# A GRU, attention and AUGRU kernel: the GRU phase in written order, attention taken out a step later, one softmax for both halves

## The chip, the cores and the metric

The kernel runs on one core of a Trainium2 chip. The metric is the device time of one execution in microseconds (us). The kernel before takes 2262.76 us, the median of 3 runs (2262.09 to 2263.09).

## What is computed

A recommendation model for 1024 users (B), each with a history of 100 items (T) of 128 numbers (D), a 0/1 mask and a length between 1 and 100. Everything is float32. Cut to its core, with `sig` for the sigmoid:

```python
hist_sum = (x * mask[:, :, None]).sum(1) / length          # [B, D]
for t in range(T):                                          # GRU over the history
    r, z = sig(Wr x_t + Ur h + b), sig(Wz x_t + Uz h + b)
    n = tanh(Wn x_t + b + r * (Un h + b'))
    h = (1 - z) * n + z * h;  keys[:, t] = h
feat = [keys, q, keys - q, q * keys]                        # q: the item, for all t
score = mlp(feat, 512 -> 80 -> 40 -> 1, relu)               # relu after each layer
attn = softmax(where(mask == 1, score, -inf), over t)
pooled = sum_t attn[:, t] * keys[:, t]                      # [B, 128]
att_seq = pooled.T[:T]                                      # the weight of step t is pooled[:, t]
for t in range(T):                                          # AUGRU over the keys
    r, u = sig(Wr [h, k_t] + b), sig(Wu [h, k_t] + b)
    c = tanh(Wh [h * r, k_t] + b)
    u = att_seq[t] * u;  h = (1 - u) * h + u * c;  seq[:, t] = h
out = mlp([user, q, hist_sum, q * hist_sum, seq[:, length - 1]], 640 -> 200 -> 80 -> 1, sig)
```

The AUGRU weights of a user depend on the pooled keys of the whole history, so no AUGRU step can begin before the last GRU step, its attention score and the last softmax are done.

## The kernel before

The users are two halves of 512. A tile is [128 features, 512 users]. A float32 matmul shows as two matmul instructions in the trace.

**GRU phase** (`gru_phase`, with one `Half` object for each half). The loop over the 100 steps issues for each half: the loads of x (`load`, L434) and of the broadcast mask row (`load_mask`, L439) for two steps ahead on SP's queue; `gru` (gates on PE at L463: r, the state part of n, the input part of n, z; ACT at L475, L480, L494; DVE at L483 to L498); `product` (L530: state times item) and `transpose` (L507: the state into rows of users, stored to DRAM as keys at L513 or L518) of the step before; after the second half `attend` of the step before; one pending softmax stage; `history` (L450, L451: GpSimd adds x times mask); and `pool` (L619, L620 on GpSimd: keys times exponents, added up, two keys a call).

`attend(t)` packs the three layers of the score network of three different steps into one PSUM tile of each half (L679, 32-column matmuls beside each other): layer 1 of step t, layer 2 of t-1, layer 3 of t-2. At once behind it DVE adds the item's part (L703), ACT applies relu (L704) and `score` sends the score row from ACT's queue to the score tile `s_b` (L540).

The softmax runs over blocks of steps (`ENDS`, mostly 8 steps, shifted by 4 between the halves, the last block 2 steps) with a running maximum `top` and sum `den`. Its two stages per half (`scores`: transpose, mask, maximum, Exp on ACT at L579; `sums`) are queued and one is issued after each half's step. An old block's pooled sum is rescaled at L605.

`load_later` is a generator; from step 2 on one piece of it is issued per step. It makes the mask tables, the lengths, the rank of each user by length (L347), the scatter of the ranks (L359), the index tables, and loads the AUGRU weights. In these pieces a conversion or a comparison on DVE often stands right behind the transfer that brings its input.

After the loop come `attend(T)` and `attend(T + 1)` for the last layers, the last stages, the rest of the pooling, `weights` (L629 to L635: pooled sums divided by `den`, stored to `pooled_d`), and `features` (L641 to L664: the parts of the last network that need no AUGRU).

**The order of the instructions.** The kernel is written for a scheduler: it takes the program as a graph and chooses each engine's order itself, by its own simulated times. Each engine then runs its list strictly in order; a wait holds all that stands behind it.

**AUGRU phase** (`augru_phase`). The users are sorted by length, longest first, so step t needs only the first `widths[t]` columns of each half: 512 at step 1, about 5 fewer each step, down to 16 (WIDTHS[0]; two wider tables stand in branches for other data). Keys are gathered from DRAM in the sorted order on GpSimd's queue (L128 for steps 0 to 7, L152 for later ones, paced by a copy of a gate at L151, `RATE` = 2 per half and step) in groups of 8 steps, and transposed on PE (L819) or DVE (L823). `sort_weights` gathers the pooled rows (L128 `att_r`), transposes them (L789) and stores them (L792); `load_att` reads back a broadcast row for a step (L806). `step` (L834, L835 on PE; L840 to L848 on ACT; L841 to L851 on DVE) uses gate tiles from a ring of 8 in PSUM; `predict` runs the last network for 128 users whenever they have finished.

## Time and profile before

| | us |
|---|---|
| the profiled execution | 2262.48 |
| its span (first to last instruction) | 2260.6 |
| PE matmuls busy | 2124.9 |
| DVE busy | 1728.9 |
| GpSimd (POOL) busy | 1285.2 |
| ACT busy | 868.3 |
| mean granted TensorE clock | 0.96 of full |

By stretches of the span: the GRU phase reaches to about 1530, the change-over to about 1602 (first matmul of AUGRU step 1), the AUGRU steps to 2247, the last network to 2261.

How to read it: "PE" is the matrix engine, "PEld" its weight loads, "DVE" VectorE, "ACT" ScalarE, "POOL" GpSimd and "SP" the engine whose queue issues most transfers. A name such as `ps<-x,wih` says that a tile `ps` is written from `x` and `wih`. Busy time on PE is not work at full speed: at a granted clock of 0.5 the same matmuls take longer and still count as busy. In the table of stretches each engine has its busy time and, in brackets, its instructions; then come the granted clock, the mean busy share of the transfer engines and GB/s. In the waits, "A <- B: us, times, longest" says that engine A stood idle until B; a wait for several events is put down to the last.

### The profile page before, as it was taken

Reading aid. Unit: us, or ns where it says so; the run is one execution under the profiler, and the core shown is the slowest. Engines: PE = TensorE matmul, PEld = TensorE weight load, DVE = VectorE, ACT = ScalarE, POOL = GpSimd, SP = SyncE. Lnnn points to the kernel's source line nnn. Section 1 sums busy time; section 2 is a strip of 40 time slices with the busy share of each in tenths; the row PEclk is TensorE's granted clock in tenths of the full one; section 3 lists DMA queues with packets and bytes.
Section 4 is the critical chain, followed back from the end, with each engine's and each line's share of the span. In section 5 each row is a group of like instructions: output and inputs, shape, how many; then the busy total and the mean of one; then the engine's idle time right before and its main releaser. Section 6 shows DMA issues by size and latency. Waiting matters only on the chain. (4 is left out here: it accounts for less than half of the span.)

```text
span 2260.6 us, 26532 instructions
## 1 busy us (share of the span) xinstructions
PE 2124.9 (94%) x8260; PEld 1013.4 (45%) x8260; DVE 1728.9 (76%) x3166; ACT 868.3 (38%) x1545; POOL 1285.2 (57%) x1289
## 2 busy tenths in 40 slices
PE   8898688999999999999999999995899999999998
PEld 3333233333333333333333333332444555679888
DVE  6776667788888888787878787898467877879752
ACT  3233223343433334333333333442343444445542
POOL 0147597676767676767676767694544444443410
PEclk9999899999999999999999999998899999999975
DMA  5344433332332323232323233312533333333310
GB/s 116 64 90 129 127 94 108 99 96 86 95 92 84 105 70 115 74 115 71 109 78 98 77 94 90 92 45 72 149 93 108 97 89 98 101 96 80 82 37 5
DMA packets 253427, 204.64 MB, mean 91 GB/s; under 512 B 74727, under 2 KB 215755, under 8 KB 253275
## 3 DMA queue, kind: packets, MB, share of 16 engines
q1 hardware_dynamic: 239482, 169.03, 27.7%
q0 software_dynamic: 12192, 32.17, 4.9%
q10 hardware_dynamic: 1600, 1.64, 0.2%
q8 instruction: 67, 1.10, 0.2%
q14 instruction: 86, 0.70, 0.1%
HBM read 146.73 MB, written 54.40 MB: 89 GB/s over the span
## 5 line engine op out<-in xcount | busy, mean ns | idle before, releaser
L463 PE MATMUL ps<-x,wih 128*128 128x512 f32 x1200 | 604.1, 613 | 62.2 <-ACT r L475 29.0
L463 PE MATMUL ps<-hn,whh 128*128 128x512 f32 x1188 | 583.2, 600 | 1.3 <-DVE hn L498 1.3
L463 PEld LDWEIGHTS ps<-x,wih 128*128 128x128 f32 x1200 | 220.0, 192 | 396.1 <-issue 214.1
L463 PEld LDWEIGHTS ps<-hn,whh 128*128 128x128 f32 x1188 | 228.4, 193 | 294.0 <-issue 267.6
L704 ACT ACTIVATE mv<-f 128x512 f32<-128x512 f32 (+1 forms) x204 | 128.2, 629 | 495.3 <-DVE f L703 371.7
L450 POOL TENSOR_TENSOR xm<-x,m 128x512 f32<-128x512 f32 x200 | 249.1, 1262 | 102.1 <-PE ps L463 72.6
L494 ACT ACTIVATE ps<-ps,bih 128x512 f32<-128x512 f32 x200 | 132.2, 661 | 400.7 <-DVE ps L493 324.4
L620 POOL TENSOR_TENSOR pooled<-pooled,kw 128x512 f32<-128x512 f32 x190 | 262.9, 1383 | 6.9
L451 POOL TENSOR_TENSOR hist<-hist,xm 128x512 f32<-128x512 f32 x200 | 263.7, 1333 | 2.9
L496 DVE TENSOR_TENSOR d<-hn,ps 128x512 f32<-128x512 f32 x198 | 135.7, 685 | 165.4 <-ACT ps L494 161.5
L605 POOL TENSOR_TENSOR pooled<-pooled,e 128x512 f32<-128x512 f32 x25 | 29.8, 1193 | 366.4 <-ACT e L579 366.4
L679 PE MATMUL pm<-hn,wk 128*32 128x512 f32 x1200 | 230.5, 600 | 6.0 <-DVE f L703 3.4
L152 POOL DMA_INDIRECT rows<-keys_d,idx_k x204 | 196.3, 962 | 69.3 <-issue 35.5
L679 PE MATMUL pm<-kq,wkq 128*32 128x512 f32 x1200 | 227.4, 594 | 0.0
L679 PE MATMUL pm<-mv,w 128*32 128x512 f32 (+1 forms) x808 | 213.5, 606 | 13.4 <-ACT mv L704 10.6
L530 DVE TENSOR_TENSOR kq<-hn,item 128x512 f32<-128x512 f32 x200 | 205.9, 1035 | 4.5 <-PE pm L679 4.3
L619 POOL TENSOR_TENSOR kw<-kt,e 128x512 f32<-128x512 f32 x190 | 207.4, 1110 | 0.5 <-DVE old L586 0.3
L483 DVE SCALAR_TENSOR_TENSOR u<-ps,bhh,r 128x512 f32<-128x512 f32 x198 | 145.8, 737 | 62.9 <-ACT r L475 53.7
L151 POOL COPY rows<-u 128x1 f32<-128x1 f32 x200 | 30.7, 181 | 258.4 <-DVE u L845 257.9
L497 DVE TENSOR_TENSOR d<-ps,d 128x512 f32<-128x512 f32 x200 | 137.9, 689 | 16.0 <-ACT ps L480 0.9
L493 DVE TENSOR_TENSOR ps<-ps,u 128x512 f32<-128x512 f32 x200 | 138.9, 694 | 13.5 <-PE ps L463 0.5
L835 PE MATMUL ph<-r,wh 128*128 128x512 f32 (+55 forms) x396 | 137.1, 430 | 9.5 <-DVE r L841 7.9
(154 smaller groups left out, 3167.0 us busy)
## 6 DMA issues: line engine op xcount, KB each, us to landing
x<-in_hist_x SPq DMA_DIRECT2D x212, 256.0 KB
keys_d<-kt SPq DMA_DIRECT2D x46, 1024.0 KB
m<-mask_d SPq DMA_DIRECT2D x200, 128.0 KB
keys_d<-kt SPq DMA_DIRECT2D x64, 64.0 KB
rows<-keys_d,idx_k POOLq DMA_INDIRECT x204, 2.8
s_b<-mv ACTq DMA_DIRECT2D x200, 8.0 KB
mask_i<-in_mask SPq DMA_DIRECT2D x8, 200.0 KB
at<-att_d SPq DMA_DIRECT2D x4, 256.0 KB
```

Source lines behind the costliest of these rows:

```text
L152: nc.gpsimd.indirect_dma_start(out=r[:, k, :], out_offset=None, in_=keys_d[q], in_offset=bass.IndirectOffsetOnAxis(ap=idx_k[:, k, i : i + ...
L450: nc.gpsimd.tensor_mul(d, x, m)
L451: nc.gpsimd.tensor_add(acc, acc, d)
L463: nc.tensor.matmul(p, lhsT=w[:, g, :], rhs=v, start=(j == 0), stop=(j == len(parts) - 1),)
L483: nc.vector.scalar_tensor_tensor(out=u, in0=ph, scalar=bhh[:, 2:3], in1=r, op0=ALU.add, op1=ALU.mult,)
L493: nc.vector.tensor_add(pi, pi, u)
L497: nc.vector.tensor_mul(d, pz, d)
L530: nc.vector.tensor_mul(kq, h, item[:, self.cols])
L619: eng.tensor_mul(d, k, w)
L620: eng.tensor_add(acc, acc, d)
L679: nc.tensor.matmul(p[i][s, :], lhsT=w[:, s], rhs=v, start=start, stop=stop)
L835: nc.tensor.matmul(p, lhsT=m[:, 0, :], rhs=v, start=False, stop=True)
```

## The change

**Order.** The GRU phase is put under `tc.manual_schedule()`: each engine gets its instructions in the order in which they are written. The AUGRU phase is still scheduled. The loop is rewritten for that order: `gru` calls `after_gate` behind the first gate of the first half and `after_sum` behind the tanh; z's sigmoid stands behind the tanh.

**Attention a step later.** `attend(t)` only issues the matmuls. `take(t)`, one step later, adds the item's part for both halves, applies relu and sends the score rows, now from SP's queue.

**Softmax of both halves at once.** One list of blocks (ends 8, 16, ... 88, 92, 96, 100) for both halves, three stages in three steps: the first half's scores; the second's scores, the maxima and differences; the sums. The Exp is issued at the end of the step. The last block has 4 steps.

**Preparation.** The attention weights are made after step 0. `load_later` starts with step 1, issues a piece only in steps without a softmax stage, and puts a piece's transfer and its use into different steps; conversions move from DVE to ACT, `ident` into a later piece.

**Change-over.** rlen and user are loaded two steps before the end; the cross features are made on GpSimd in step 99; the 8 feature groups stand between the last attention layers. Half 1's remaining keys are pooled on DVE, half 0's last block is split: 11 of 16 column blocks on GpSimd, 5 on DVE. The weights are built in the score tiles. In AUGRU the keys of steps 0 and 1, the first step's gates and step 1's input matmuls come before `sort_weights`. One or two keys a call are pooled in the loop; the history of steps 0 to 5 is made up from step 24 on instead of 12.

**AUGRU.** Gates use 6 PSUM tiles, everything else 2 of its own. The gathers of a group are spread evenly over the steps before it and end a step early (`spread`, for `RATE`). No width is below 96 (`LEAST`).

```diff
-ENDS = ((*range(8, 89, 8), 92, 96, 98, T), (*range(4, 93, 8), 96, 98, T))
+ENDS = (*range(8, 89, 8), 92, 96, T)
-RATE = 2
-EIGHTH, FALL = 8, 41
+EIGHTH, FALL, LEAST = 8, 41, 96
+    [max(LEAST, min(HB, 2 * -(-r // (2 * EIGHTH)))) for r in room] for room in ROOM
...
             def gru(self, t, after_gate, after_sum):
                 nc.scalar.activation(r, pr, AF.Sigmoid, bias=brz[:, 0:1])
+                after_gate()
...
-                nc.scalar.activation(pz, pz, AF.Sigmoid, bias=brz[:, 1:2])
...
                 nc.scalar.activation(pi, pi, AF.Tanh, bias=bih[:, 2:3])
+                nc.scalar.activation(pz, pz, AF.Sigmoid, bias=brz[:, 1:2])
+                after_sum()
...
+        def take(t):
+            p = left.pop(t)
+            for half in halves:
+                if t < T:
+                    sums.append(wp.tile([P, HB], F32, name="f"))
+                    nc.vector.tensor_add(sums[-1], p[half.i], q0[:, half.cols])
+            for half in halves:
+                    nc.scalar.activation(to, sums[half.i], AF.Relu)
...
+            for half in halves:
+                nc.sync.dma_start(out=s_bs[...], in_=half.mv[SC[half.i] : SC[half.i] + 1, :]...)
+            if s == blocks[j + 1] - 1:
+                softmax()
...
         for s in range(T):
+            def after_gate():
+                take(s - 2)
+                for half in halves:
+                    half.product(s - 1)
+            for half in halves:
+                half.gru(s, after_gate if s and half.i == 0 else nothing,
+                    (lambda: half.transpose(s - 1)) if s else nothing)
+                if half.i == 0:
+                    staged = bool(soft["stages"])
+                    stage(2 if last else 1)
+            exponents()
+            if s == 0:
+                attention_weights()
+            else:
+                if not staged:
+                    next(rest, None)
+                attend(s - 1)
...
+        cut = KH // 3
+        parts = (
+            ((nc.gpsimd, slice(cut, KH)), (nc.vector, slice(0, cut))),
+            ((nc.vector, slice(0, KH)),),
+        )
...
-        ps = pools.enter_context(tc.tile_pool(name="ps3", bufs=8, space=PSUM))
+        ps = pools.enter_context(tc.tile_pool(name="ps3", bufs=6, space=PSUM))
+        pa = pools.enter_context(tc.tile_pool(name="pa3", bufs=2, space=PSUM))
...
         for i in range(NH):
+            load_key(1, i)
+            open_gates(1, i)
+        for i in range(NH):
             sort_weights(i)
...
-                for _ in range(RATE):
+                for _ in range(due.pop(0) if due else 0):
                     next(ahead, None)
...
-    with ExitStack() as pools:
+    with ExitStack() as pools, tc.manual_schedule():
         gru_phase(pools)
```

More of the change, by code (lines that the diff above doesn't have):

```diff
@@ L742, in gru_phase, with some @@
+        all_of(rest)
+        features = [half.features(g) for half in halves for g in range(GH)]
+        def some(these):
+            for f in these:
+                next(f)
+        halves[0].pool(T, pool_part)
+        take(T - 2)
         for half in halves:
             half.product(T - 1)
+        attend(T - 1)
+        some(features[:2])
+        for half in halves:
             half.transpose(T - 1)
-        attend(T - 1)
-        for half in halves:
-            while half.stages:
-                half.stage()
@@ L749, in gru_phase @@
[L749 to L759 removed]
+        halves[1].pool(1, (nc.vector, slice(0, KH)))
+        take(T - 1)
+        some(features[:2])
+        attend(T)
+        some(features[2:4])
+        halves[1].pool(1, (nc.vector, slice(0, KH)))
```

530 lines of the change are left out of this document (296 added, 234 removed).

## The prediction

> **What bounds the kernel now.** I read the page first, then stretches of the span by engine, then the pace of single steps, then the waits.
>
> ```profile
> span 2260.6 us, 26532 instructions
> PE 2124.9 (94%) x8260; PEld 1013.4 (45%) x8260; DVE 1728.9 (76%) x3166; ACT 868.3 (38%) x1545; POOL 1285.2 (57%) x1289
> ...
> PE   8898688999999999999999999995899999999998
> ...
> PEclk9999899999999999999999999998899999999975
> ```
>
> TensorE is the busiest engine everywhere. There are two kinds of exceptions: the first seven slices and the 28th and 29th, where PE waits, and the last two, where PE looks nearly full but the granted clock falls. The profiled execution took 2262.48 us, 1.88 outside its span; the median of the runs is 2262.76, so the sum is made on 2260.6 and 1.88 is added at the end.
>
> The stretches; 41.89, 447.19 and 1529.47 are the starts of the attention groups of steps 1, 24 and 98, the later ones are ends or clock changes of the AUGRU phase:
>
> ```profile
> core 0: us, PE busy (x) PEld busy (x) DVE busy (x) ACT busy (x) POOL busy (x), PEclk, DMA share, GB/s
> 41.89:447.19 405.30, 353.16 (x1305) 133.31 (x1304) 288.33 (x443) 129.12 (x199) 233.27 (x192) 0.93 0.42 103
> 447.19:1529.47 1082.28, 1059.88 (x4145) 404.49 (x4145) 899.89 (x1378) 420.03 (x649) 763.24 (x616) 1.00 0.31 89
> 694.72:765.06 70.34, 70.34 (x281) 27.07 (x280) 60.50 (x94) 28.07 (x44) 40.07 (x33) 1.00 0.32 95
> 1529.47:1602.49 73.02, 43.36 (x180) 21.44 (x180) 46.15 (x106) 20.39 (x37) 37.96 (x34) 0.78 0.27 74
> 2168.07:2181.30 13.23, 11.14 (x89) 10.09 (x87) 8.10 (x44) 6.00 (x22) 0.00 (x0) 1.00 0.09 22
> 2181.30:2246.85 65.55, 64.06 (x287) 61.59 (x286) 22.55 (x140) 20.08 (x74) 2.23 (x4) 0.50 0.04 9
> 2246.85:2260.63 13.78, 5.33 (x21) 4.03 (x20) 0.00 (x1) 2.35 (x7) 1.97 (x2) 0.50 0.03 7
> ```
>
> And the pace of one GRU step, from the start of one attention group on PE to the next (timeline):
>
> ```profile
> 796.12 0.62 PE L679 MATMUL pm<-hn,wk 128*32 128x512 f32 x2
> ...
> 810.19 0.62 PE L679 MATMUL pm<-hn,wk 128*32 128x512 f32 x2
> ...
> 1529.47 0.62 PE L679 MATMUL pm<-hn,wk 128*32 128x512 f32 x2 [1.43 <-DVE e L569]
> ```
>
> An undisturbed step takes 14.07 us. A step issues 56 matmuls (24 at L463, 32 at L679). The second stretch holds 4145, that is 74 steps; the first holds 1305, of which 16 belong to `count` (L272), that is 23 steps. At 14.07 they would take 1041.2 and 323.6. The excess is 41.1 us in the second and 81.7 in the first, 122.8 together. The third row is five clean steps: PE is busy throughout, DVE 60.50/5 = 12.1 us a step, POOL 8.0. So PE's own work is the floor, and the excess is time in which PE lacked an input.
>
> What it lacked, from the waits, one row of ACT's timeline, and the waits of SP's queue between 200 and 260:
>
> ```profile
> ACT mv L704 <- DMA m<-mask_d: 82.8, 19, 5.9
> ...
> 238.50 0.63 ACT L704 ACTIVATE mv<-f 128x512 f32<-128x512 f32 x1 [14.52 <-DMA len_k<-in_len_i]
> ...
> SPq L434 <- POOL xm L450: 32.0, 4, 13.8
> ```
>
> ACT does no loads of x or masks, yet it waits for their transfers: it issues the score transfer (L540), and that issue stands in ACT's queue until an earlier transfer has ended. In the row of 238.50 this held ACT, and with it the gates, for 14.5 us.
>
> **The change, part by part.** *GRU in program order.* Inside a step no matmul is added or removed, so the floor stays 14.07. The score transfers go from ACT's queue to SP's. Behind them on SP stand the next step's x and mask loads, which are issued two steps before use, about 28 us; a score transfer waits only for a relu early in its step. I expect no one to miss them. ACT then queues arithmetic only. DVE's queue becomes, per step: two sums of the attention taken out, two products, then for each half gate product, sum, transpose of the last step, three state operations. The new waits are those at its head (the attention group of the step before, which PE has just ended) and those for ACT. Queued behind are the states of both halves; PE works in order through 12 gate matmuls a half and the attention group (14.07 shared over 24 gate matmuls and 32 that run four abreast is 0.44 each, an estimate: 5.3 us a half, 3.5 the group), so it needs each half's state some 6 to 7 us after DVE makes it. So a DVE lag of some 6 us costs nothing. Durations:
>
> ```profile
> L530 DVE TENSOR_TENSOR kq<-hn,item 128x512 f32<-128x512 f32 x200 | 205.9, 1035 | 4.5 <-PE pm L679 4.3
> L619 DVE TENSOR_TENSOR kw<-kt,e 128x512 f32<-128x512 f32 x8 | 5.5, 684 | 2.8 <-POOL pooled L620 2.8
> L619 POOL TENSOR_TENSOR kw<-kt,e 128x512 f32<-128x512 f32 x190 | 207.4, 1110 | 0.5 <-DVE old L586 0.3 <-DVE e L582 0.2
> L620 POOL TENSOR_TENSOR pooled<-pooled,kw 128x512 f32<-128x512 f32 x190 | 262.9, 1383 | 6.9
> L450 POOL TENSOR_TENSOR xm<-x,m 128x512 f32<-128x512 f32 x200 | 249.1, 1262 | 102.1 <-PE ps L463 72.6 <-DMA over_d<-over_i 19.3 <-DMA m<-mask_d 5.7
> L475 ACT ACTIVATE r<-ps,brz 128x512 f32<-128x512 f32 x200 | 136.3, 681 | 24.3 <-PE ps L463 23.9
> L579 ACT ACT_TABLE_LOAD x26 | 33.4, 1283 | 27.0 <-DVE e L574 26.7
> L272 PE MATMUL count<-alive,ones 128*1 128x100 f32 x16 | 2.8, 371 | 4.8 <-DVE own L339 4.8
> ```
>
> DVE has 14.07 - 12.1 = 2 us a step to spare, and a later softmax stage (two transposes and small operations, about 2.3) overruns by well under 6. POOL per step: history four operations of about 1.3 = 5.2, pooling of one key a half 2 x (1.11 + 1.38) = 5.0, so 10.2 of 14.07; two keys a half make 15.2, in one step of eight and again from step 92. Its lag at step 99 is then some 10 us, and the cross features (four more, 5 us) now stand in its queue ahead of half 0's last pooling; both lie under the attention layers of the change-over, and would add up to 10 us there if those were quicker. *Softmax of both halves at once* halves the 26 Exp table loads (1.28 each) and sets them behind the step's last gate on ACT; before, they stood between gates. *The preparation* issues a transfer in one step and uses it in the next, with its conversions on ACT, so DVE no longer stands before a transfer. The attention weights are made after step 0, where DVE and PE meet them in order: step 1's attention about 1 us later. I keep 7 of the 122.8 us (`count` 2.8, this 1, the rest an estimate): **-116**. Ends: -122.8 (all goes) and -75 (41.1 + 7 stays).
>
> *The change-over.*
>
> ```profile
> 1577.31 6.58 SPq L635 DMA_DIRECT2D pooled_d<-att  x8
> ...
> 1586.17 2.08 PE L777 MATMUL pu<-k,wu 128*128 128x512 f32 x2 [12.62 <-ACT k L820]
> ...
> 1586.21 0.99 POOL L128 DMA_INDIRECT att_r<-pooled_d,idx  x1 [28.03 <-DMA pooled_d<-att]
> ...
> 1604.36 0.66 PE L835 MATMUL pr<-h,wr 128*128 128x512 f32 x1
> ...
> 1616.80 0.69 DVE L851 TENSOR_TENSOR h<-h,ph 128x512 f32<-128x512 f32 x1
> ```
>
> Now it is 1586.21 - 1529.47 = 56.7 us from the start of attention step 98 to the first gather of the sorted weights, and 31.3 more to the end of AUGRU step 1. After the change the features fill PE while the last attention layers wait for each other, and the last softmax covers both halves: from the start of step 98's group I count 3.5 for it, 5 for the last state, relu and product, 3 x about 5 for the layers and their sums, 6 for transfer, scores and sums: about 30. But the last block has 4 steps, not 2. DVE pools half 1 with 9 operations of 0.68 to 1.04, 6.1 to 9.4, beside POOL's share of half 0 (11 of 16 columns of 1.1 + 4 x 2.5, 7.6), then 5/16 of 9 operations and two products, 3.5; then about 4.5 from the last store to the gather as now. That makes 44 to 47.5. The row kq, beside a busy POOL, takes 1.035 where L619 on DVE, with POOL idle, takes 0.684, so I take the slower end.
>
> The Trainium skill, GPSIMD Engine Reference, section Specifications, says why: GpSimd shares SBUF interfaces with VectorE and collides with DVE instructions that read two SBUF inputs; this speaks against pooling on both at once, and by it the 9 operations cost 3.2 us more than alone; the two rows agree.
>
> So the gather comes about 9 us sooner. Keys of steps 0 and 1 and step 1's three input matmuls a half no longer wait (row 1586.17), but PE comes back at the low clock: 5 us of the 31.3. **-14**, ends -4 (stores late, cold clock) and -22.
>
> *AUGRU.* Gate slots go from 8 to 6, exactly one step's gates, with prediction on 2 of its own; PE is full here and the next step's gates reuse slots long read: 0, ends -6 and +6. The gathers are spread so that they end a step before their keys are used. Four stalls stand there:
>
> ```profile
> 1685.24 0.67 PE L834 MATMUL pr<-k,wr 128*128 128x482 f32 x1 [1.54 <-DVE k L823]
> ...
> 1888.80 0.58 PE L835 MATMUL ph<-r,wh 128*128 128x370 f32 x1 [1.96 <-DVE r L841]
> ```
>
> The others are near the lesser of these, about 6 in all: **-4**.
>
> *Least width 96.* Ends of the steps of width 98, 92, 88, 82, 72, 66 and 16 on DVE:
>
> ```profile
> 2167.82 0.25 DVE L851 TENSOR_TENSOR h<-h,ph 128x98 f32<-128x98 f32 x1
> ...
> 2171.25 0.25 DVE L851 TENSOR_TENSOR h<-h,ph 128x92 f32<-128x92 f32 x1
> ...
> 2174.70 0.23 DVE L851 TENSOR_TENSOR h<-h,ph 128x88 f32<-128x88 f32 x1
> ...
> 2178.60 0.23 DVE L851 TENSOR_TENSOR h<-h,ph 128x82 f32<-128x82 f32 x1
> ...
> 2188.94 0.23 DVE L851 TENSOR_TENSOR h<-h,ph 128x72 f32<-128x72 f32 x1
> ...
> 2194.89 0.22 DVE L851 TENSOR_TENSOR h<-h,ph 128x66 f32<-128x66 f32 x1
> ...
> 2246.68 0.17 DVE L851 TENSOR_TENSOR h<-h,ph 128x16 f32<-128x16 f32 x1
> ```
>
> The steps of 92 and 88 take 3.43 and 3.45, that of 82 takes 3.90, all at clock 1.00; that of 66 takes 5.95, at clock 0.50. So a wider step is the faster one as long as the clock holds. The 16 steps from 84 on take 78.8; at 3.43 to 3.90 they take 55 to 62, and I take 58: **-21**.
>
> Sum: 2260.6 - 116 - 14 - 4 - 21 = 2105.6, with 1.88 outside **2107**.
>
> **Rivals.** *The clock does not hold.* Between 2168 and 2181 PE was busy 11.14 of 13.23 us and still lost the clock at 2181.3, so width, not idle time, seems to decide; 96 is between 98 and 92, which kept it, but they were passed in single steps. Without it 16 steps take about 6.0, 96 us, 17 more than now: 2107 + 21 + 17 = 2145.
>
> The Trainium skill, TensorE: Matmul & The Clock Gate, section "What's actually happening", has the clock halved after an idle window of about 3.4 us; by that, padding changes nothing, and the result would be this rival's; the trace differs, since PE had no such gap there.
>
> *Softmax stalls stay.* If the 41.1 us come from DVE work and table loads and not from where they stand: 2107 + 34 = 2141. Against it: half the table loads go.
>
> *SP takes over ACT's wait.* SP waited 13.8 us for POOL's history to free x; a score transfer behind it now holds DVE at the softmax, in order. If the first stretch keeps its 81.7: 2107 + 75 = 2182. Against it: history no longer lags in the preparation.
>
> *DVE becomes the bound: slower.* In program order DVE may stand out each gate, tanh and sigmoid of ACT, six of about L475's 0.68, 4.1 us on top of 12.1: 16.2 a step. Then 97 steps take 1571 instead of 1488: 2107 + 116 + 83 = 2306. The change is lost from 15.7 us a step on ((1488 + 39)/97). Against it: transposes and stages lie in these gaps, and other work of ACT and PE runs ahead by half a step.
>
> **How the numbers follow.** Forecast 0.59, clock 0.12, softmax 0.14, SP 0.08, DVE 0.06, no gain at all 0.01. The time is that of the forecast. Its own ends, all gains full and everything small late, are about 2084 and 2125; the range reaches to the clock's and softmax's cases: 2082 to 2150. About 0.2% (4.5 us) is what a measurement can tell: faster 0.93, same 0.01, slower 0.06.
>
> **What would show it.** Right: attention groups 14.07 apart from step 2 to 98 with the softmax steps no longer; no ACT wait on transfers; the start of group 98 near 1412; the first gather of weights some 48 us later; PEclk 1.00 to the last AUGRU steps, each 3.4 to 3.9. Wrong: steps of 15 us or more with PE waiting for DVE; SP's queue waiting for POOL; clock 0.50 from about 80 us before the end.

## The result, and the profile after

| | before | after | forecast |
|---|---|---|---|
| median, us | 2262.93 (4 runs) | 2149.37 (4 runs, 2148.13 to 2156.20) | 2107 |
| span of the profiled execution | 2260.6 | 2148.5 | 2105.6 |

The ratio is 0.9505, 95% interval 0.9485 to 0.9525: clearly faster, by 113.6 us where 155.8 were forecast. The time lies at the very end of the range, beyond the forecast's own ends (2084 to 2125) and nearest to what the clock's and the softmax's rivals would have given (2145 and 2141). Neither of these happened, as the traces below show, so that nearness is luck.

The page of the kernel after:

```profile
span 2148.5 us, 26525 instructions
PE 2048.8 (95%) x8260; PEld 977.8 (46%) x8260; DVE 1766.3 (82%) x3034; ACT 829.1 (39%) x1509; POOL 1290.2 (60%) x1296
...
PE   8999999997999999999999999984999999999886
...
PEclk9999999998999999999999999996999999999998
```

The holes of the first seven slices are gone but for the first; the hole at the change-over (slices 27 and 28) is not, and one new digit 7 stands in the tenth slice. At the end PE is less full than before, at a higher clock. The same stretches as before the change: attention groups 1 to 24, 24 to 98, then to the first gather of sorted weights, to the end of AUGRU step 1, and, after a gap, steps 84 to 99 and the tail:

```profile
core 0: us, PE busy (x) PEld busy (x) DVE busy (x) ACT busy (x) POOL busy (x), PEclk, DMA share, GB/s
45.55:371.60 326.05, 325.91 (x1305) 126.72 (x1304) 285.43 (x421) 122.43 (x196) 176.73 (x144) 1.00 0.41 102
371.60:1435.54 1063.94, 1045.56 (x4146) 401.31 (x4146) 930.78 (x1315) 392.43 (x623) 813.04 (x661) 0.99 0.34 98
1435.54:1498.47 62.93, 30.78 (x152) 17.94 (x152) 47.22 (x70) 10.33 (x21) 30.93 (x27) 0.74 0.22 56
1498.47:1528.68 30.21, 26.18 (x71) 12.18 (x72) 11.20 (x18) 12.47 (x19) 23.33 (x26) 0.86 0.56 166
2074.61:2134.16 59.55, 47.78 (x379) 44.99 (x377) 40.52 (x185) 27.52 (x96) 9.22 (x16) 0.97 0.24 37
2134.16:2148.49 14.33, 5.35 (x22) 3.90 (x20) 0.00 (x0) 2.60 (x8) 1.97 (x2) 0.53 0.03 6
```

The first row took 405.30 and takes 326.05, 2.4 above the floor of 23 x 14.07. The second took 1082.28 and takes 1063.94, 22.8 above its floor. The third and fourth together took 88.0 and take 93.1. Two places need a closer look. The first is step 35, in DVE's and PE's timelines:

```profile
525.15 0.73 DVE L702 STREAM_TRANSPOSE pt<-s_b 128x512 f32<-128x512 f32 x1 [14.41 <-DMA s_b<-mv]
...
526.35 1.03 PE L626 MATMUL pm<-mv,w 128*32 128x512 f32 x1 [13.00 <-DVE e L706]
```

DVE stands 14.4 us at the head of a softmax stage for a score transfer, and 1.2 us later PE's wait of 13.0 ends on it. What SP did meanwhile, from its timeline and its queue's waits between 440 and 560:

```profile
501.41 0.41 SPq L452 DMA_DIRECT2D m<-mask_d  x1
521.71 0.33 SPq L447 DMA_DIRECT2D x<-in_hist_x  x1
...
522.57 1.13 SPq L674 DMA_DIRECT2D s_b<-mv  x2
```

```profile
SPq L447 <- POOL xm L463: 54.4, 8, 19.3
```

SP issued nothing for 20 us: an x load (L447) waited for GpSimd's history to free a tile, and the score transfer (L674) was issued only behind it. Step 35 lost 16.2 us so, step 43 lost 4.3; another 2.5 lie in steps 97 and 98.

The second place is the change-over; PE, DVE and GpSimd:

```profile
1434.41 0.72 DVE L702 STREAM_TRANSPOSE pt<-s_b 128x512 f32<-128x512 f32 x1
...
1442.38 0.69 DVE L514 TENSOR_TENSOR hn<-ps,d 128x512 f32<-128x512 f32 x1
1443.11 0.59 DVE L723 TENSOR_TENSOR e<-e,on 128x128 f32<-128x128 f32 x1
...
1446.13 1.27 DVE L660 TENSOR_TENSOR f<-pm,q 128x512 f32<-128x512 f32 x2
...
1446.86 1.07 PE L626 MATMUL pm<-hn,wk 128*32 128x512 f32 x2 [6.84 <-DVE f L660]
...
1455.60 1.55 DVE L567 TENSOR_TENSOR kw<-kt,e 128x512 f32<-128x512 f32 x1 [2.31 <-POOL pooled L568]
...
1458.74 1.28 DVE L660 TENSOR_TENSOR f<-pm,q 128x512 f32<-128x512 f32 x2
...
1477.28 0.35 DVE L730 RECIPROCAL den<-den 128x32 f32<-128x32 f32 x1
...
1483.63 1.18 POOL L567 TENSOR_TENSOR kw<-kt,e 128x352 f32<-128x352 f32 x1 [6.69 <-DVE pooled L568]
...
1498.47 0.99 POOL L133 DMA_INDIRECT att_r<-pooled_d,idx  x1 [6.39 <-DMA pooled_d<-s_b]
```

Step 99's attention group starts after 6.84 us without a matmul. On DVE two softmax stages of the block that ends at 96 (from 1434.41 on) stand ahead of the second half's last state (1442.38), and the third (from 1443.11 on) ahead of the sums (1446.13) that PE waits for. The sums of step 99's group (1458.74) stand behind a pooling operation that waits for GpSimd, and GpSimd's share of the split pooling waits 6.69 us for DVE: they take turns in the two kw tiles. The last sums of the softmax, to the end of RECIPROCAL, come 42.1 us after step 98's group began (30 forecast), the first gather comes 20.8 later (17.5 forecast).

### The profile page after: what moved, and what is told of

Same layout as the page of the kernel before. It is cut to its first block, busy times and chain, and to the rows that moved or that the text cites. A ratio compares the mean times of both kernels' runs of the same rounds, so it can differ in the third digit from the quotient of the medians.

```text
span 2148.5 us, 26525 instructions
## 1 busy us (share of the span) xinstructions
PE 2048.8 (95%) x8260; PEld 977.8 (46%) x8260; DVE 1766.3 (82%) x3034; ACT 829.1 (39%) x1509; POOL 1290.2 (60%) x1296
## 5 line engine op out<-in xcount | busy, mean ns | idle before, releaser
L477 PE MATMUL ps<-x,wih 128*128 128x512 f32 x1200 | 593.2, 603 | 4.7 <-DMA x<-in_hist_x 4.2
L489 ACT ACTIVATE r<-ps,brz 128x512 f32<-128x512 f32 x200 | 137.4, 687 | 396.2 <-PE ps L477 394.8
L568 POOL TENSOR_TENSOR pooled<-pooled,kw 128x512 f32<-128x512 f32 (+1 forms) x190 | 253.4, 1334 | 14.9
L567 POOL TENSOR_TENSOR kw<-kt,e 128x512 f32<-128x512 f32 (+1 forms) x190 | 217.8, 1146 | 71.6 <-DVE e L723 64.7
L546 DVE TENSOR_TENSOR kq<-hn,item 128x512 f32<-128x512 f32 x200 | 231.7, 1198 | 0.0
L626 PE MATMUL pm<-hn,wk 128*32 128x512 f32 x1200 | 216.3, 603 | 8.5 <-DVE f L660 6.8
L626 PE MATMUL pm<-mv,w 128*32 128x512 f32 (+1 forms) x808 | 203.2, 611 | 19.8 <-DVE e L706 16.2
L626 PE MATMUL pm<-kq,wkq 128*32 128x512 f32 x1200 | 213.2, 597 | 0.0
L660 DVE TENSOR_TENSOR f<-pm,q 128x512 f32<-128x512 f32 x200 | 128.5, 684 | 56.7 <-PE pm L626 56.7
L560 POOL TENSOR_TENSOR pooled<-pooled,e 128x512 f32<-128x512 f32 (+1 forms) x24 | 25.6, 1066 | 199.9 <-ACT e L720 199.9
```

The costliest lines, as they stand in the source:

```text
L477: nc.tensor.matmul(p, lhsT=w[:, g, :], rhs=v, start=(j == 0), stop=(j == len(parts) - 1),)
L489: nc.scalar.activation(r, pr, AF.Sigmoid, bias=brz[:, 0:1])
L546: nc.vector.tensor_mul(kq, h, item[:, self.cols])
L567: eng.tensor_mul(d, k, w)
L568: eng.tensor_add(acc, acc, d)
L626: nc.tensor.matmul(p[i][s, :], lhsT=w[:, s], rhs=v, start=start, stop=stop)
```

## The experiments

Each starts from the changed kernel. A difference of medians is given between kernels that ran on the same chip, and for another chip of the same kind (by the time of the kernel before) only where the text says so; positions in the traces are given from the start of attention step 98. The kernel before took 2262.9 beside the first result, 2257.1 beside the second series (perhaps on the same chip) and 2297.7 to 2302.9 on four other chips; the last experiment deals with that. On those four, ACT and DVE stand still for some us behind the start of the AUGRU phase, which is called the still stretch below. Ratios are to the kernel before on the same chip, with their intervals. Up to the first gather the positions agree from chip to chip: in three traces of the changed kernel, one of them from one of the four, groups 1 to 98 take 1390.0 to 1392.0 us and the first gather comes 61.6 to 62.9 after group 98. A difference of about 1 us there means little.

**The changed kernel once more,** run after four of the experiments below, which are those that its expectation speaks of.

> The changed kernel itself once more, as the measure for the three beside it, since the kernel before ran 37 us longer beside the first four experiments than beside the changed kernel. If the chip is one like the first: 2149 and a ratio of 0.9505. If those 37 us, and the 15 to 17 us more that the first four took from the first gather of the sorted weights to the end of AUGRU step 1, belong to the chip and not to their edits: about 2170 to 2185, with the same stretch longer here.

Measured 2150.73, ratio 0.952 (0.9489 to 0.9552); step 98 at 1437.57, the excesses of steps 35 and 43 16.2 and 6.2. It is the measure for three runs that follow.

**The order alone undone.**

```diff
-    with ExitStack() as pools, tc.manual_schedule():
+    with ExitStack() as pools:
         gru_phase(pools)
```

> The changed kernel's program, but the GRU phase is left to the scheduler, as in the kernel before. Order theory (the gain of the GRU phase is the order: no instruction that waits for a transfer ahead of gates): attention groups again have 80 to 120 us of excess over 14.07, attention step 98 starts near 1510 to 1530, about 2230 to 2250. Rival, contents theory (the later take-out, the common softmax and the preparation that puts a transfer and its use into different steps do it under any order): within 10 us of the copy of the changed kernel.

Measured 2252.49, ratio to before 0.9964 (0.9944 to 0.9984), 101.8 more than the changed kernel beside it. Step 98, and what DVE's transposes of the scores waited for:

```profile
1538.84 0.62 PE L626 MATMUL pm<-hn,wk 128*32 128x512 f32 x2
```

```profile
DVE pt L702 <- DMA x<-in_hist_x: 40.6, 4, 10.8
```

Without the written order nothing of the GRU phase's gain is left: the new program under the scheduler reaches group 98 9 us later than the old one did beside the first result. Whether the old program, put in written order, would gain as much was not run. Group 1 starts at 41.79 in this run, as before the change: that it starts at 45.6 in the changed kernel is also the order, PE meeting the item's projection ahead of step 1's gates.

**Loads behind the score transfers, or GpSimd relieved.**

```diff
             def after_gate():
                 take(s - 2)
+                for half in halves:
+                    if s + AHEAD < T:
+                        half.load(s + AHEAD)
...
```

These loads no longer stand at the head of the step.

> The changed kernel, but the x and mask loads of a step are issued behind the score transfers of that step on SP's queue instead of ahead of them; GpSimd's work is untouched. Queue theory (a score transfer stands behind an x load that waits for GpSimd's history to free a tile, and DVE, in program order, waits for the score): the attention groups of steps 35 and 43 come 14.07 after the one before, as the others do; 16.2 + 4.3 = 20 us go, about 2129. Rival, GpSimd theory (its list is full in steps 24 to 47, and DVE or PE wait for something that GpSimd itself makes or frees): nothing changes, 2149. Third, the preparation's own transfers hold DVE: nothing changes either.

```diff
-            n, odd = divmod(s - again, 2)
+            n, odd = divmod(s - again, 4)
...
-            if 0 <= n < late and odd:
+            if 0 <= n < late and odd == 1:
```

> The changed kernel, but the history of steps 0 to 5 is made up every fourth step (24 to 71) instead of every second (24 to 47); the order on SP's queue is untouched. Queue theory: GpSimd's list has 0.65 us less to do per step there (one pair of operations of 1.2 + 1.3 in four steps instead of two), x tiles come free earlier, and the stalls of steps 35 and 43 shrink to a third or less: 2129 to 2136, with perhaps a smaller one later. GpSimd theory: the same. Third theory, that the scatters of the ranks or the index tables hold DVE whatever the history does: 2149.

Measured 2154.56 and 2154.77, with before at 2300.11: ratios 0.9373 (0.9357 to 0.9389) and 0.9367 (0.935 to 0.9384). The stalls of steps 35 and 43 are gone in both. From group 1 to group 98 they take 1366.5 and 1368.5 us, the changed kernel 1390.0 to 1392.0, the floor is 1364.8. Some of the gain is lost again: the first gather comes 65.2 and 64.0 after group 98 here. Beside the changed kernel on a chip of the same kind (2170.85, last experiment) both are some 16 us faster, where 20, and 13 to 20, were expected. SP's whole waits for GpSimd, in the changed kernel and with the loads behind:

```profile
SPq L447 <- POOL xm L463: 130.0, 27, 19.3
```

```profile
SPq L447 <- POOL xm L463: 58.8, 8, 15.4
```

SP still waits up to 15.4 us, and now nobody misses it. With the loads behind, GpSimd has as much to do as before, so the account that GpSimd's list alone holds DVE or PE falls. GpSimd is the start of the chain, and the order on SP's queue hands its lag to DVE.

**The score transfers back on ACT's queue.**

```diff
-                nc.sync.dma_start(out=s_bs[...], in_=half.mv[...])
+                nc.scalar.dma_start(out=s_bs[...], in_=half.mv[...])
```

> The changed kernel, but the score transfers are issued from ACT's queue, as in the kernel before, and everything else stays in written order. Queue theory: no x load stands ahead of them there, so the stalls of steps 35 and 43 go as with the loads put behind, 20 us less than the copy of the changed kernel, about 2129; ACT pays about 0.6 us per issue, for which it has room. Rival (ACT's issue itself waits until earlier transfers have ended, as the row of 14.52 us in the trace of before was read): ACT stands before the gates and 20 to 80 us come, 2170 or more.

Measured 2183.93, ratio 0.9503 (0.9478 to 0.9528), and step 98 at 1450.03, some 13 us later than in the changed kernel: the queue theory missed. The rival named the right wait, at a smaller price than its 20 to 80 us. SP's loads and ACT around step 35:

```profile
525.59 0.33 SPq L447 DMA_DIRECT2D x<-in_hist_x  x1
...
526.49 0.38 SPq L447 DMA_DIRECT2D x<-in_hist_x  x1
...
530.29 1.19 ACTq L674 DMA_DIRECT2D s_b<-mv  x2
531.52 0.66 ACT L508 ACTIVATE ps<-ps,bih 128x512 f32<-128x512 f32 x1 [15.56 <-DMA s_b<-mv]
```

The score transfers go out only as SP's held loads go out, though they are on another queue. The semaphore events in the trace say why (a semaphore is a counter by which a transfer tells that it has landed). The transfers of SP and ACT use the same eight semaphores in turn. The first score transfer goes out at 530.29; the x load of 526.49, which used its semaphore before it, gives its last signal at 530.22. For the second these are 530.98 and 530.90. So here a transfer goes out only when the one that last used its semaphore has landed, whatever its queue. A held x load holds the scores on either queue; on ACT it holds the gates as well. In the kernel before SP and ACT share eight semaphores too, and ACT's wait of 14.52 us ends in the same way: the score transfer goes out at 237.90, the len_k load that used its semaphore before it gives its last signal at 237.82.

**The stages behind, and tiles of its own.**

```diff
-                    stage(2 if last else 1)
+                    stage(0 if last else 1)
             exponents()
-            if last:
-                stage()
...
-        halves[0].pool(T, pool_part)
...
-        halves[1].pool(1, (nc.vector, slice(0, KH)))
         take(T - 1)
+        stage(2)
+        exponents()
...
+        take(T)
+        stage()
+        halves[0].pool(T, pool_part)
         halves[1].pool(1, (nc.vector, slice(0, KH)))
-        take(T)
```

> The changed kernel, but the three softmax stages of the block that ends at 96 stand on DVE behind the state of step 99 and the sums of attention steps 98 and 99, not ahead of them, and the pooling that needs them behind that. DVE-list theory (the stages ahead of the last state, then the sums of step 98 and a pooling operation that waits 2.3 us for GpSimd, made the three attention groups start late and at the low clock): attention step 99 starts about 7 us sooner at the full clock, the sums of attention 99 some 11 us sooner, the first gather of sorted weights about 10 us sooner (6 to 14), about 2139. Rival, pooling bounds (DVE has 18 operations of half 1 and 9 narrow ones of half 0 to do between the stages and the store, whatever the order): 2 to 4 us, about 2146.

```diff
-                            d = wp.tile([P, KH, R], F32, name="kw")[:, part, :]
+                            tag = "kw" if eng is nc.gpsimd else "r"
+                            d = wp.tile([P, KH, R], F32, tag=tag, name="kw")[:, part, :]
```

> The changed kernel, but DVE's pooling writes its products to tiles of its own (the tag of r, free by then) and GpSimd's keeps the two of kw. Ring theory (in the change-over the two engines take turns in a ring of two tiles, so DVE waits 2.3 us for GpSimd at 1455 and GpSimd 6.7 us for DVE at 1483, and the split runs one after the other): both waits go, GpSimd's share ends some 6 us sooner, DVE's pooling of half 1 becomes slower beside it (9 operations from 0.69 to 1.04, 3 us), the first gather comes 3 to 5 us sooner; 3 to 5 less than the copy of the changed kernel. Rival, DVE alone bounds and contention eats it: 0 to 1 less.

> Both edits: the three softmax stages behind the last sums, and tiles of its own for DVE's pooling. In the run with the stages behind alone the last two attention layers were done at 1456.7, but DVE stood 5.9 us for a kw tile that GpSimd held, and the last transpose came only at 1469.4. Ring theory: from the start of attention step 98 to the first gather 60.2 us become about 48 (9 from DVE's wait, 3 from the split), 12 less than with the stages behind alone and 15 less than the copy of the changed kernel. Rival, pooling bounds whatever the tiles: 2 to 4 less than with the stages behind alone.

In us from the start of attention step 98 (the median apart):

| | attention 100 starts | last sums end | first gather | median | ratio |
|---|---|---|---|---|---|
| changed kernel | 24.6 | 42.1 (41.2 in the second trace) | 62.9 (62.0) | 2150.73 | 0.952 (0.9489 to 0.9552) |
| stages behind | 14.6 | 39.4 | 60.2 | 2172.59, another chip | 0.9451 (0.9435 to 0.9467) |
| tiles apart | 22.2 | 37.7 | 57.5 | 2146.75 | 0.9511 (0.9479 to 0.9543) |
| both | 14.7 | 37.8 | 57.6 | 2146.32 | 0.9501 (0.9469 to 0.9533) |

With the stages behind, the attention layers come 10 us sooner, as expected, and nearly all of it is lost again ahead of the last softmax: the first gather comes 2 to 3 us sooner, not 10, as the rival had it. With tiles apart both waits go and the gather comes 4.5 us sooner, as expected. Both together do no more than that: the 12 us of my ring theory did not come, the rival held. DVE and GpSimd with tiles apart:

```profile
1477.64 1.28 DVE L568 TENSOR_TENSOR kw<-kt,e 128x512 f32<-128x512 f32 x1
...
1482.70 0.68 DVE L568 TENSOR_TENSOR kw<-kt,e 128x512 f32<-128x512 f32 x1
...
1472.84 0.79 POOL L568 TENSOR_TENSOR kw<-kt,e 128x352 f32<-128x352 f32 x1
...
1477.13 1.24 POOL L568 TENSOR_TENSOR kw<-kt,e 128x352 f32<-128x352 f32 x1
```

The same DVE operation takes 1.28 us while GpSimd pools and 0.68 when it has ended; GpSimd's takes 0.79 and 1.24. The Trainium skill, SBUF — State Buffer, section "Who interferes with whom", calls the port pair that the two share an exclusive lock. The trace agrees in part: side by side each takes far longer than alone, but less than the 1.47 us that the two would take one behind the other.

Side by side both engines start an operation every 1.27 us; alone, DVE starts one every 0.67. At that pace DVE would do its own 512 columns and GpSimd's 352 in 1.12 us, an estimate from these two paces. So the split gains nothing.

**Less help, and the chain first.**

```diff
-            ((nc.gpsimd, slice(cut, KH)), (nc.vector, slice(0, cut))),
+            ((nc.vector, slice(0, KH)),),
             ((nc.vector, slice(0, KH)),),
```

> The changed kernel with tiles of its own for DVE's pooling, and half 0's last block pooled by DVE alone: GpSimd does nothing after the last softmax. Port theory (beside GpSimd a DVE operation with two inputs from SBUF takes 1.28 instead of 0.69, and GpSimd's own 1.24 instead of 0.79, so two engines do no more than DVE alone): from the start of attention step 98 to the first gather 56 to 57.5 us, as with the split (57.5) or up to 1.5 less. Rival, the split helps as it is meant to: DVE has 9 operations of 0.33 more to do, so 60 to 61.

```diff
         halves[0].pool(T, pool_part)
-        halves[1].pool(1, (nc.vector, slice(0, KH)))
...
-        halves[1].pool(1, (nc.vector, slice(0, KH)))
         take(T + 1)
-        halves[1].pool(T, (nc.vector, slice(0, KH)))
```

> The run with the stages behind and tiles of its own, and the rest of half 1's older keys pooled by DVE behind the last softmax instead of ahead of it. DVE-list theory (the last scores stand behind that pooling): the last sums end about 29 us after the start of attention step 98 instead of 38, and the first gather comes 6 to 9 us sooner, 49 to 52 after it. Pooling theory (the same operations have to be done before the store, wherever they stand): the sums come sooner, the first gather 0 to 3 us sooner, 55 to 58.

Measured 2169.05 and 2167.78 with before at 2302.88: 0.9416 (0.938 to 0.9452) and 0.942 (0.9384 to 0.9456), no clear difference from the changed kernel's 0.9447 on a chip of this kind; the positions have to tell. The ends of the last sums and the first gathers, with DVE alone (step 98 at 1436.08):

```profile
1472.67 0.35 DVE L731 RECIPROCAL den<-den 128x32 f32<-128x32 f32 x1
...
1491.91 0.99 POOL L133 DMA_INDIRECT att_r<-pooled_d,idx  x1 [32.66 <-DMA pooled_d<-s_b]
```

and with the chain first (step 98 at 1434.10):

```profile
1463.79 0.35 DVE L731 RECIPROCAL den<-den 128x32 f32<-128x32 f32 x1
...
1484.99 0.69 DVE L863 TENSOR_TENSOR s_b<-s_b,pooled 128x512 f32<-128x512 f32 x1
...
1489.95 0.99 POOL L133 DMA_INDIRECT att_r<-pooled_d,idx  x1 [17.64 <-DMA pooled_d<-s_b]
```

With GpSimd idle behind the last softmax the gather comes at 55.8, 1.7 sooner than with the split. The rival's 60 to 61 is out: the help brought nothing, and a small loss is likely but hardly clear of the spread between traces. With the chain first the last sums end at 30.0, 8 sooner than with both edits before it, and the gather comes at 55.9, 1.8 sooner than there. DVE works without a gap from those sums to the last product (1485.68), 4.3 us ahead of the gather: the pooling bounds, wherever it stands.

**The least width undone.**

```diff
-EIGHTH, FALL, LEAST = 8, 41, 96
+EIGHTH, FALL, LEAST = 8, 41, 2
```

> The changed kernel with the least width 2 in place of 96 (the last steps go down to 16 users a half again). Clock theory (below a width of 70 to 80 the granted clock falls to half, whatever else changed): the 16 steps from 84 on take the 78.8 of the kernel before instead of 56 to 60, 19 to 22 us more than the copy of the changed kernel, about 2170, and PEclk 0.5 to the end. Rival (the clock fell before because prediction and gathers stood in the way; with tiles of its own and spread gathers it holds): the narrow steps run at full clock, at 3.0 to 3.4 each as the latency of the chain has it, about 50, 2140 to 2146.

Measured 2195.12, ratio 0.9545 (0.9529 to 0.9561). From the end of step 83 to the end of step 99 it takes 82.3 us; the changed kernel took 59.6, and three other runs with width 96 on this run's chip 57.8 to 64.5. So the width is worth 18 to 25 us there, the clock theory held and its rival did not. PE's row at the end of step 86, and the stretch from there on:

```profile
2107.39 0.71 PE L958 MATMUL pr<-h,wr 128*128 128x78 f32 x2 [2.43 <-DVE h L974]
```

```profile
2109.63:2177.96 68.33, 65.34 (x297) 63.73 (x297) 24.80 (x147) 20.54 (x76) 2.31 (x4) 0.50 0.04 9
```

**The four edits, and the first matmuls ahead.** The four are loads behind, history every fourth step, stages behind and tiles apart. The second adds:

```diff
+        with tc.manual_schedule():
             for i in range(NH):
                 load_key(0, i)
...
             for i in range(NH):
                 sort_weights(i)
```

> The changed kernel, but the first part of the AUGRU phase, up to and with sort_weights, is put in program order too, so that PE's list has the first step's and step 1's input matmuls ahead of the transposes of the sorted weights. List theory (those matmuls had no reason to wait; they stood behind two transposes that wait for the gather): the 8 + 12 matmul instructions, about 14 us at the low clock, run under the store and the gather, step 1 ends 8 us sooner (6 to 10), about 2141. Rival, the chain of the weights alone bounds (gather, transposes, copy, store and reading back of the broadcast row of step 1): 2147 to 2149. A second rival, that the scheduler's order of the rest gets worse: slower by up to 5.

> Four edits at once: x and mask loads behind the score transfers, history made up every fourth step, softmax stages behind the last sums, tiles of its own for DVE's pooling. If they add: 22 us of stalls in steps 35 and 43 and 2.4 in 97 and 98 go, 4 to 5 in the change-over, so 25 to 29 less than the copy of the changed kernel, about 2124 (2120 to 2128). Rival: the history that is made up later (to step 71) makes GpSimd late elsewhere, and 5 to 8 come back: 2130.

> As the run with the four edits, and the first part of the AUGRU phase in program order too. List theory: the first step's and step 1's input matmuls run under the store and the gather and step 1 ends 6 to 9 us sooner than with the four edits alone, about 2116. Rival, seen beside the earlier run of this edit on another chip: ACT stood 13.2 us with its input ready and then, with DVE, 2 to 5 us at a time up to step 2, without any releaser in the trace, so that what PE gains is lost there: 0 to 2 less, or some us more.

> The run with the four edits, with the older keys behind the last softmax and the last block pooled by DVE alone. Pooling and port theories together: 1 to 4 us less than with the four edits, a first gather 52 to 56 us after attention step 98 (55.8 there). On a chip like the first: 2120 to 2126; on one where ACT and DVE stand still behind the branch, about 15 more.

> The run before, and the first part of the AUGRU phase in program order. On a chip without the still stretch list theory has AUGRU steps 1 and 2 end 6 to 9 us sooner than in the run before, counted from the first gather; on one with it, step 1 ends some 10 us sooner and step 2 takes some 10 more, so nothing is left.

In the last column, in us: the time from the first gather to the end of AUGRU step 1, and the time of step 2. The last row has all edits.

| | chip's before | median | ratio | first gather to end of step 1, step 2 |
|---|---|---|---|---|
| first matmuls ahead alone | 2300.11 | 2171.93 | 0.944 (0.9422 to 0.9458) | 38.3, 14.5 |
| four edits | 2299.57 | 2140.68 | 0.9317 (0.9294 to 0.934) | 44.0, 9.4 |
| and first matmuls ahead | 2299.57 | 2143.17 | 0.9315 (0.9294 to 0.9335) | 33.2, 19.2 |
| four, chain first, DVE alone | 2302.88 | 2143.38 | 0.9316 (0.9281 to 0.9351) | 46.9, 9.4 |
| and first matmuls ahead | 2302.88 | 2142.39 | 0.9298 (0.9258 to 0.9337) | 36.3, 17.5 |

The first matmuls put ahead take 10.6 to 10.8 us off step 1 and give 8 to 10 back in step 2, so nothing measurable is left on these chips, as the rival had it. That edit has not run on a chip of the other kind. The four edits do add up: in them the group of step 98 comes 14.07 after the one before and starts at 1413.03, and the first gather comes 55.8 later; the ratio is 0.9317 where the changed kernel has 0.9447 on a chip of the same kind.

**The changed kernel and all edits, side by side.**

> The changed kernel once more beside the kernel with all edits. Chip theory: if the kernel before takes some 2300 here, this one takes about 2172 (2149 + 15 in the change-over + 6 to 10 in the AUGRU steps), with ACT and DVE standing still after the first gather; if it takes 2257 to 2263, about 2150 and no such stretch. Rival, that the edits made it: 2150 beside a kernel before of 2300.

> The kernel with all edits beside the changed kernel. The stalls (24), the change-over's 9 and the first matmuls' 6 to 9 on a chip without the still stretch: 36 to 42 less than the changed kernel, about 2110. On a chip with it 28 to 32 less, about 2142.

Measured 2170.85 for the changed kernel (ratio 0.9447, 0.9412 to 0.9481), with before at 2297.7, and 2141.73 for all edits (0.9316, 0.9282 to 0.9349), 29 us less, as expected for such a chip. All edits together make the changed kernel 1.3% faster; the four edits alone have as good a ratio. DVE in the changed kernel on this chip, at the sorted weights of the second half:

```profile
1525.83 0.69 DVE L903 COPY att_t<-pw 128x512 f32<-128x512 f32 x1 [9.92 <-remote]
```

Here DVE stands 9.9 us and the trace names no instruction that released it, and from the first gather to step 1's end it takes 42.9 us (30.2 in the first result). The semaphore events say a little more. DVE's copy starts 0.03 us behind a signal of PE at 1525.80. In the first result's trace the signals of the transposes that it waits for come 0.11 us apart, up to 1516.83; here signals come 1.4 to 2.8 us apart, and some are missing. No transfer that brings instructions is recorded between 1500.8 and 1534.4, so late code is not seen as the reason. The unedited kernel has the stretch here and has none in the first two traces, so it belongs to the chip, not to the edits.

## Why the prediction was wrong, step by step

Two terms failed: the GRU phase gained 22 us less than forecast, because score transfers were held behind loads, and the change-over became 5 us longer instead of 14 shorter, because of the work and the waits on DVE ahead of the first gather and a wait on PE behind it.

| term | forecast | measured |
|---|---|---|
| GRU phase, to the start of attention 98 | -116 | -93.9 |
| change-over, to the end of AUGRU step 1 | -14 | +5.1 |
| AUGRU steps 2 to 83 (gathers -4, slots 0) | -4 | -4.7 |
| least width, steps 84 to 99 | -21 | -19.2 |
| after the last step | 0 | +0.6 |
| sum | -155 | -112.1 |

**Floor and order: right.** The groups are 14.07 apart nearly everywhere, softmax steps included; the first stretch's excess fell from 81.7 to 2.4. It takes the order, as the run without it shows. The softmax steps are no longer than others, so the rival "Softmax stalls stay" did not come true. "DVE becomes the bound" did not come true.

**"I expect no one to miss them": wrong, 20.5 us.** Score transfers on SP stand behind x loads, and the argument was that these are issued 28 us before use. True, but a load that is early for its reader can still be late for what stands behind it. The rival "SP takes over ACT's wait" named the mechanism; I set it aside because "history no longer lags in the preparation". It lags while the history is made up (steps 24 to 47), at about a quarter of that rival's price of 75. Two runs that undo it in different ways take all of it away. And "ACT then queues arithmetic only" was read too simply: ACT's old wait was for a load that SP issued late, as the semaphores show, so moving the transfer to SP left its cause in place.

**"Step 1's attention about 1 us later": 3.7**, by the order.

**The change-over: wrong, 19 us.** Of these, 12.1 came before the last sums, 3.3 from there to the first gather, 3.9 behind it. (1) The 30 us to the last sums became 42.1: on DVE two stages of the block before stand ahead of step 99's last state, the third ahead of the next sums, then pooling with a wait for GpSimd's kw tile. The 30 are reached (30.0) once the chain is put first. (2) "DVE pools half 1 with 9 operations" counted only the last block: the block before it, 92 to 95, is pooled in the change-over as well, another 9 operations for each half. Nine at 0.69 are 6.2 us, and the best first gather is 53.5 after step 98 (all edits), 6.0 above the 47.5: this is the term that no order removed. The price beside GpSimd was also off. I took 1.035 from the row kq as the contended one; that row is a mean of 58 operations without GpSimd beside them (0.67 on average) and 142 with (1.18). In the changed kernel half 1's last 9 operations took 6.5 us, most of them at 0.68, because GpSimd stood waiting for a tile. DVE's share of half 0, now beside GpSimd, then took 6.8 us, and 2.7 in the run with the chain first, where GpSimd had finished. One operation of that share in the changed kernel, and in that run:

```profile
1487.44 1.08 DVE L567 TENSOR_TENSOR kw<-kt,e 128x160 f32<-128x160 f32 x1
```

```profile
1482.42 0.32 DVE L568 TENSOR_TENSOR kw<-kt,e 128x160 f32<-128x160 f32 x1
```

(3) "Keys of steps 0 and 1 and step 1's three input matmuls a half no longer wait": they did, and from the first gather to the end of step 1 it takes 30.2 us, where 26.3 were forecast. The scheduler orders that phase, and it put two transposes of sorted weights, which wait for the gather, ahead of them on PE:

```profile
1501.15 0.44 PE L901 MATMUL pw<-ident,att_r 128*128 128x128 f32 x1 [23.61 <-issue]
...
1502.60 1.92 PE L888 MATMUL pu<-k,wu 128*128 128x512 f32 x2
```

What these matmuls would bring on a chip without the still stretch was not measured.

**Slots and gathers: the number right, the reason not.** Steps 2 to 83 take 4.7 us less where 4 were forecast, but PE's idle time there, which the four stalls were part of, did not fall:

```profile
1617.49:2168.07 550.58, 537.17 (x2108) 357.52 (x2107) 428.46 (x982) 249.56 (x527) 229.39 (x402) 1.00 0.35 93
```

```profile
1528.68:2074.61 545.93, 530.78 (x2098) 356.10 (x2097) 425.09 (x979) 246.45 (x524) 230.15 (x400) 1.00 0.35 95
```

It was 13.4 us (first row, before) and is 15.2 (second, after): new stalls came, one of them 3.55 us long. The gain is in PE's busy time, and its cause is open; that the number fits is luck.

**Width: right** within 2 us, with the clock at 0.97 on average in those steps. The rival "the clock does not hold" did not come true, though a dip remains (last section).

## What to carry to other kernels

In written order, ask of every wait what is queued behind it, and of every load whether it can be held by a tile that a slow engine frees; put what is urgent ahead of what is early. Count the work that a phase leaves over for its end by the list of what is pending there, not by the last block alone. Before an engine's work is split over DVE and GpSimd, compare their times side by side with one of them alone.

## What the runs showed of the hardware that was not expected

On four chips ACT, and in most runs DVE too, stood still behind the start of the AUGRU phase, in all fourteen runs there, without a releaser in the trace. The two longest waits of the run with least width 2:

```profile
ACT pr L963 <- remote: 13.6, 1, 13.6
DVE att_t L903 <- remote: 12.0, 1, 12.0
```

None of the other six traces has it. On those four chips the kernel before was some 35 to 46 us slower, the changed one, on the one of them where it ran, some 21, of which some 12 lie in this stretch. The cause is open.

The clock: with least width 2, after PE's gap of 2.43 us (above), the granted clock was 0.50 for 68 us and never rose, though PE counts as busy for 65.34 of them. In the first trace of the changed kernel a gap of 2.80 us at width 96 cost one dip; the rows of PE behind it and of two stretches:

```profile
2086.63 0.46 PE L958 MATMUL pr<-h,wr 128*128 128x96 f32 x2 [2.80 <-DVE h L974]
```

```profile
2086.63:2091.00 4.37, 4.37 (x24) 4.37 (x24) 2.10 (x11) 1.76 (x6) 0.00 (x0) 0.61 0.11 19
2092.20:2130.00 37.80, 31.59 (x263) 29.89 (x261) 27.08 (x123) 18.91 (x66) 6.91 (x12) 1.00 0.24 36
```

In all eighteen traces with width 96 PE has such a gap there, of 1.5 to 3.0 us. The clock then stood at half for anything from nothing to 17.07 us, 3.41 in this one, and came back each time; at the lesser widths, in the kernel before and with least width 2, it stayed at half to the end, 81.4 and 87.8 us. The longest dip of the changed kernel, in its last trace, but for its first 3.7 us:

```profile
2105.21:2118.54 13.33, 12.51 (x58) 12.02 (x57) 6.02 (x27) 4.11 (x14) 2.31 (x4) 0.50 0.16 25
```

The Trainium skill, TensorE: Matmul & The Clock Gate, section "What's actually happening", has the full clock back after a busy window of about 3.4 us. The first trace at width 96 agrees; the one above (PE busy for 12.51 of 13.33 us at half the clock) and the two at lesser widths do not, if what the profile calls busy is what the page means.
